# Block sizes 6, 10, 16 in place of 4, 9, 19 in a graph-attention and quantile kernel

## The chip, the cores and the metric

The kernel runs on one core of a Trainium2 chip. A core has a matrix engine (PE, with its weight loads shown as PEld), a vector engine (DVE), a scalar engine (ACT), GpSimd (POOL), and a queue that only issues transfers (SP). The engines run side by side and wait for one another through semaphores. The metric is device time in microseconds, lower is better: the median of three runs of the kernel before is 4632.38 us (4607.63 to 4632.42).

## The reference

There are 4096 nodes of 128 features and a 4096 x 4096 adjacency matrix of which about one entry in 128 is set, some 32 neighbours a row. Two layers are computed.

```python
# layer 0: graph attention with 8 heads, then ELU, a projection, ELU, residual and layer norm
Wh = einsum('nd,hde->hne', nodes, W)
e = leaky_relu(f1[:, :, None] + f2[:, None, :], 0.2)        # f1 = Wh.a1, f2 = Wh.a2
att = softmax(where(adj > 0, e, -9e15), axis=-1)
h = elu(einsum('hnm,hmd->hnd', att, Wh))
x = layernorm(nodes + elu(concat(h) @ W1 + b1))
# layer 1: of each node's neighbours one or two are removed by their rank; for each feature the
# quantiles 0.25, 0.5 and 0.75 over the rest are averaged
agg = 0.5 * mean_of_quantiles + 0.5 * x
out = agg @ W.T + b + x
```

## The kernel before, in words

The rows are worked on in 32 tiles of 128 nodes. The kernel never forms the 4096 x 4096 attention. It finds each node's neighbours as a list of up to 64 indices and gathers the neighbours' rows.

**Search.** `neighbours` (line 568) reads a tile's adjacency rows in two halves by the ACT queue, turns them into signs on ACT, forms sortable keys on PE (lines 625 and 628) and picks the largest ones on DVE, eight at a time: `eights` over chunks of 128 columns (line 592), then eight rounds of `best` (lines 597 and 599). Line 643 is the last step of a tile. `complete_records` (line 649) then finishes the lists of a group of up to four tiles. The function is a generator: it yields `pieces_of(n)` pieces (line 564), which the caller deals out among other work.

**Ranking and blocks.** The nodes of a block of tiles are sorted by their number of neighbours. `rank_by_count` (line 704) works out ranks, and `store_records` (line 391) gives the scatters on the POOL queue that write each node's record (list, count, own index, attention terms, row) to its rank in DRAM. Sorted, the nodes of a tile have nearly equal counts, so a tile needs as many gather slots as its largest count. `CAPS` (line 44) holds that limit for each tile of a block; a count above it raises a flag (line 805), for which a general and much longer path (lines 501 to 503) computes everything again. `BLOCKS` (line 53) holds the blocks' sizes, `TURNS` (line 56) the order in which a block's tiles are taken.

**Attention.** For a sorted tile, `read_lists` (line 796) reads the records back by SP and transposes the lists into index columns. `layers` (line 90) cuts the limit, rounded up to a multiple of four, into layers of 32, 32, 16, 8 or 4 slots. `fetch_rows` (line 847) issues one indirect gather on POOL for every slot (128 rows each) into buffers `G` of 16 slots, six of them. `attend` (line 873) computes scores and Exp (line 894), the denominators (lines 901 and 916), spreads the weights (line 932), multiplies them with `G` on PE (line 944), and does the projections and the norm; `keep_x1` scatters the result.

**Order.** The instruction order of DVE, PE, ACT and POOL is written by hand from line 398 on. The first block is searched before anything else. Then, for each block, `step` (line 357) issues the gathers of one tile, the attention of the tile before it, and between these a quota of pieces of the next block's search. Before a block's last tile the next block's search ends and its ranks are computed; that block's record scatters go among the last tile's gathers. In the last block there is no search: all nodes are ranked together, scatters to `all_d` lie among the gathers of most tiles, and the lists of layer 1 are made in the last four tiles.

**Sort.** The second half gathers the neighbours' layer-0 rows by the lists of all nodes and runs a selection network on DVE (line 1155) for the quantiles; lines 455 to 497. It uses the limits of the entry `32` of `CAPS`, which stay as they are.

Of the kernel before, what the change touches and what calls it, by code (L numbers as in the profile page):

```python
# [41 lines left out]


CAPS = {
    4: [29, 33, 37, 60],
    9: [26, 28, 30, 32, 33, 35, 37, 40, 61],
    19: [24, 26, 27, 28, 29, 30, 30, 31, 32, 33, 33, 34, 35, 36, 37, 38, 40, 42, 62],
    32: [
        23, 24, 25, 26, 27, 27, 28, 29, 29, 30, 30, 30, 31, 31, 32, 32,
        33, 33, 34, 34, 35, 35, 36, 36, 37, 37, 38, 39, 40, 41, 44, 63,  # L50
    ],
}
BLOCKS = [4, 9, 19]


TURNS = {4: range(4), 9: range(9), 19: [0, 1, 2, 3, 18, 4, 5, 6, 7, *range(9, 18), 8]}

CAP = CAPS[NT]
LOW = [
# [142 lines left out]
def scatter(nc, rows, src, idx):  # L202
    return nc.gpsimd.indirect_dma_start(  # L203
        out=rows,
        out_offset=bass.IndirectOffsetOnAxis(ap=idx, axis=0),
        in_=src,
        in_offset=None,
    )
# [9 lines left out]
def kernel(  # L218
# [18 lines left out]
    xt_d = dram.tile([N + P, XW], F32, name="xt_d")  # L237
    recs_d = [dram.tile([n * P, REC], F32, name=f"rec{n}_d") for n in BLOCKS]
    all_d = dram.tile([N, REC1], F32, name="all_d")
# [72 lines left out]
    def search(t0, n):  # L312
        return neighbours(
            tc, adjp, cp, kp, rec, num, adj, t0, n, parts, markb, oneb, bad, jp1, pidx
        )

    for _ in search(0, BLOCKS[0]):
        pass
# [26 lines left out]
    def prepare(b, i, t0):  # L345
        n = BLOCKS[b]
        i = TURNS[n][i]
        return read_lists(tc, attp, recs_d[b], i, CAPS[n][i], t0 + i, bad, narrow)
# [42 lines left out]
    def store_records(b, t0, ranks):  # L391

        return [
            (recs_d[b], rec[:, t0 + i, :], ranks[:, i : i + 1]) for i in range(BLOCKS[b])
        ]

    t0 = 0
    with tc.manual_schedule(engines=ORDERED):
        ranks = rank_by_count(tc, cp, kp, num, jp1, before, oneb, 0, BLOCKS[0])
        for v in store_records(0, 0, ranks):  # L400
            scatter(nc, *v)
        for b, n in enumerate(BLOCKS):
            last = b == len(BLOCKS) - 1
# [1024 lines left out]
```

## Time and profile before

| | |
|---|---|
| Median of three runs | 4632.38 us |
| Profiled execution, its own time | 3702.95 us (span 3701.2 us) |
| DVE busy | 2746.5 us, 74% |
| POOL busy | 2421.0 us, 65% |
| PE busy | 1228.3 us, 33% |
| Gathers of attention (`G`) | 1180, mean 996 ns |
| Gathers of the sort (`vals`) | 1024, mean 1027 ns |

The profiled execution is much shorter than the timed ones. Lines of the profile name an engine, an operation, what it writes and reads, how often, the busy time, the mean time of one, and the engine's idle time before it with what ended most of that. `L944` is line 944 of the kernel. A row of the view by stretches has the stretch, its length, each engine's busy time with its instruction count, the granted clock of PE, the transfer engines' share and their rate. A row of the waits has who waited, for whom, microseconds in all, how often, and the longest.

### The profile page before, as it was taken

What the parts mean: (1) busy time and instruction counts of PE and PEld (TensorE: products, weight loads), DVE (VectorE), ACT (ScalarE), POOL (GpSimd) and SP (SyncE); (2) the same over time, 40 slices, a digit from 0 to 9 for tenths busy, and PEclk for the clock granted to TensorE, in tenths of its full rate; (3) what the DMA queues carried; (4) which work ended last, traced back from release to release, by engine and by line L of the source; (5) the groups of instructions that cost most, each with busy time, mean ns of one, the idle gap of its engine ahead of it and who ended that gap; (6) DMA issues with size and microseconds to landing.
All of it is one profiled execution on the core that took longest, in us unless ns stands there. A gap on an engine that the chain in (4) does not pass through costs nothing. (4 is left out here: it accounts for less than half of the span.)

```text
span 3701.2 us, 23191 instructions
## 1 busy us (share of the span) xinstructions
PE 1228.3 (33%) x5433; PEld 936.3 (25%) x5433; DVE 2746.5 (74%) x7565; ACT 403.4 (11%) x603; POOL 2421.0 (65%) x2388
## 2 busy tenths in 40 slices
PE   6483767773673544454450000000000000000011
PEld 2043544453562443444440000000000000000011
DVE  8774688782541222127637999999999999999998
ACT  3121222220120111111110000000000000000000
POOL 1657674467777777777747777677657565667630
PEclk9975676655575555565555555555555555555555
DMA  6432544322222221222211111111111111111100
GB/s 211 156 99 67 182 137 136 128 72 62 59 54 55 53 55 52 53 66 57 55 33 49 47 47 46 43 46 46 37 38 48 36 42 40 44 44 49 42 19 3
DMA packets 110291, 241.33 MB, mean 65 GB/s; under 512 B 46976, under 2 KB 63360, under 8 KB 101952
## 3 DMA queue, kind: packets, MB, share of 16 engines
q0 software_dynamic: 76160, 160.24, 15.5%
q10 hardware_dynamic: 9360, 67.18, 5.2%
q1 hardware_dynamic: 24624, 12.34, 1.4%
q8 instruction: 45, 0.74, 0.1%
q14 instruction: 102, 0.84, 0.1%
HBM read 228.44 MB, written 11.15 MB: 65 GB/s over the span
## 5 line engine op out<-in xcount | busy, mean ns | idle before, releaser
L194 POOL DMA_INDIRECT G<-xt_d,idx x1180 | 1174.8, 996 | 478.8 <-issue 336.4
L194 POOL DMA_INDIRECT vals<-x_d,idx x1024 | 1052.1, 1027 | 337.6 <-issue 298.5
L1155 DVE TENSOR_TENSOR work<-work 128x512 f32<-128x512 f32 (+6 forms) x1405 | 961.0, 714 | 0.4
L1174 PE MATMUL st_ps<-dg,goal 128*128 128x128 f32 x286 | 71.2, 426 | 1645.3 <-DVE goal L1155 1574.9
L1155 DVE TENSOR_TENSOR work<-work,work 128x512 f32<-128x512 f32 (+5 forms) x958 | 606.4, 658 | 0.7
L1174 PEld LDWEIGHTS st_ps<-dg,goal 128*128 128x128 f32 x286 | 63.2, 322 | 1651.7 <-issue 1650.8
L944 PE MATMUL y<-wide,G 128*128 128x32 f32 (+3 forms) x2360 | 460.3, 371 | 23.9 <-DVE wide L932 23.9
L944 PEld LDWEIGHTS y<-wide,G 128*128 128x128 f32 x2360 | 440.2, 286 | 47.5 <-DVE wide L932 26.3
L887 DVE TENSOR_TENSOR z<-G,f1x 128x128 f32<-128x128 f32 (+2 forms) x92 | 29.9, 335 | 471.5 <-DMA G<-xt_d,idx 467.3
L592 DVE MAX8 first<-key 128x8 f32<-128x128 f32 x1024 | 227.8, 282 | 108.4 <-PE key L628 108.3
L203 POOL DMA_INDIRECT out_dram<-o,own_i x32 | 45.6, 1425 | 297.4 <-ACT o L1200 277.8
L625 PE MATMUL key<-sgn,markb 128*128 128x512 bf16 x256 | 141.6, 554 | 162.3 <-DVE first L592 108.9
L1126 DVE COPY junk<-still 128x1 f32<-128x1 f32 x1295 | 194.7, 150 | 0.0
L901 PE MATMUL small<-z,own 128*4 128x32 f32 (+3 forms) x436 | 50.2, 284 | 380.6 <-ACT z L894 380.6
L1155 DVE TENSOR_TENSOR work<-vals 128x1024 f32<-128x1024 f32 (+8 forms) x140 | 138.8, 1009 | 46.4 <-DMA vals<-x_d,idx 46.1
L586 ACT ACTIVATE sgn<-adj_t 128x2048 bf16<-128x2048 int32 x64 | 122.0, 1907 | 340.7 <-PE key L625 304.5
L1173 ACT ACTIVATE dg<-ident,wt 128x128 f32<-128x128 f32 x143 | 47.5, 394 | 957.2 <-PE st_ps L1174 956.8
L916 PE MATMUL rz<-rden,ownT 4*128 4x32 f32 (+3 forms) x436 | 104.7, 411 | 117.3 <-DVE rden L912 96.0
L628 PE MATMUL key<-parts,oneb 64*128 64x512 bf16 x256 | 140.4, 549 | 6.3 <-POOL parts L212 6.3
L974 PE MATMUL small<-W_sb,late 128*128 128x128 f32 x512 | 118.7, 425 | 33.5 <-DVE late L971 33.5
L901 PEld LDWEIGHTS small<-z,own 128*4 128x4 f32 x436 | 27.1, 102 | 398.1 <-ACT z L894 385.8
L916 PEld LDWEIGHTS rz<-rden,ownT 4*128 4x128 f32 x436 | 91.9, 302 | 133.5 <-DVE rden L912 68.4
(179 smaller groups left out, 1891.7 us busy)
## 6 DMA issues: line engine op xcount, KB each, us to landing
adj_t<-in_adj_dram ACTq DMA_DIRECT2D x64, 1024.0 KB
G<-xt_d,idx POOLq DMA_INDIRECT x1180
vals<-x_d,idx POOLq DMA_INDIRECT x1024
R<-rec_d SPq DMA_DIRECT2D x128, 26.2 KB
xt_d<-rec SPq DMA_DIRECT2D x4, 544.0 KB
rec<-in_x_dram SPq DMA_DIRECT2D x4, 512.0 KB
W_sb<-in_L_gnn_W_dram SPq DMA_DIRECT2D x2, 512.0 KB
a_b<-in_L_gnn_a_dram SPq DMA_DIRECT2D x2, 512.0 KB
```

The lines of the kernel that those rows point to most:

```text
L194: nc.gpsimd.indirect_dma_start(out=dst, out_offset=None, in_=rows, in_offset=bass.IndirectOffsetOnAxis(ap=idx, axis=0),)
L586: nc.scalar.activation(sgn, adj_t, AF.Sign, accum_out=cnt[:, i : i + 1])
L592: nc.vector.max(first[:, ts(c0 // CW + c, 8)], key[:, ts(c, CW)])
L625: nc.tensor.matmul(key, lhsT=markb, rhs=sgn[:, ts(b, 512)], start=True, stop=False)
L628: nc.tensor.matmul(key, lhsT=oneb[0:64, :], rhs=parts[:, ts(r, 512)], start=False, stop=True)
L901: nc.tensor.matmul(den[0:4, :].rearrange("p (g r h) -> p r g h", r=k // 4, h=H)[:, r], lhsT=own[w][:, ts(r, 4)], rhs=z[:, layer[i] : layer ...
L916: nc.tensor.matmul(rz[:, layer[i] * H : (layer[i] + w) * H], lhsT=ownT[w][:, r, :], rhs=rden.rearrange("p (g r h) -> p r g h", r=k // 4, h ...
L944: nc.tensor.matmul(yf[:, ts(g, c)], lhsT=G[:, col + g - g0, 0:D], rhs=pf[:, ts(g, c)], start=(i == 0 and g % (w // 2) == w // 2 - 1), stop ...
L974: nc.tensor.matmul(o, lhsT=hv[:, h, :], rhs=consts["W1_sb"][:, h, :], start=(h == 0), stop=(h == H - 1))
L1126: nc.vector.tensor_copy(junk, late["still"])
L1155: nc.vector.tensor_tensor(slots_of(dst, (j, c, s, m), size), slots_of(a, (i, c, s, m), size), slots_of(b, (i + d, c, s, m), size), op,)
L1174: nc.tensor.matmul(st_ps[:, u, :], lhsT=goal[:, (j * k + u) * D : (j * k + u + 1) * D], rhs=dg, start=(j == 0), stop=False,)
```

## The change

The three blocks of attention tiles get other sizes, still 32 tiles in sum, with limits and an order of tiles to match.

```diff
 CAPS = {
-    4: [29, 33, 37, 60],
-    9: [26, 28, 30, 32, 33, 35, 37, 40, 61],
-    19: [24, 26, 27, 28, 29, 30, 30, 31, 32, 33, 33, 34, 35, 36, 37, 38, 40, 42, 62],
+    6: [28, 30, 33, 35, 39, 61],
+    10: [26, 28, 30, 31, 33, 34, 36, 38, 40, 61],
+    16: [24, 26, 28, 29, 30, 31, 31, 32, 33, 34, 35, 36, 38, 39, 42, 62],
     32: [
         23, 24, 25, 26, 27, 27, 28, 29, 29, 30, 30, 30, 31, 31, 32, 32,
         33, 33, 34, 34, 35, 35, 36, 36, 37, 37, 38, 39, 40, 41, 44, 63,
     ],
 }
-BLOCKS = [4, 9, 19]
+BLOCKS = [6, 10, 16]
 
 
-TURNS = {4: range(4), 9: range(9), 19: [0, 1, 2, 3, 18, 4, 5, 6, 7, *range(9, 18), 8]}
+TURNS = {6: range(6), 10: range(10), 16: [0, 1, 2, 3, 15, 4, 5, 6, *range(8, 15), 7]}
```

Everything else follows from these tables: how many tiles are searched before the first gather, how many pieces of search go into a step, how many slots each tile gathers.

## The prediction

> **What bounds the kernel now.** I read the page's engine shares first (DVE 74%, POOL 65%: shares of stages with different limits), then cut the span where POOL, GpSimd's queue, changes its job: first gather of block 4 (113), of block 9 (362), of block 19 (929), last gather (1884), first gather of the sort (1922). Busy time by engine in each stretch:
>
> ```profile
> core 0: us, PE busy (x) PEld busy (x) DVE busy (x) ACT busy (x) POOL busy (x), PEclk, DMA share, GB/s
> 0.00:113.00 113.00, 59.43 (x168) 25.30 (x168) 81.38 (x315) 32.47 (x86) 19.56 (x28) 1.00 0.57 188
> 113.00:362.00 249.00, 151.46 (x485) 81.32 (x486) 176.18 (x704) 46.95 (x48) 173.31 (x178) 0.77 0.35 108
> 362.00:929.00 567.00, 377.03 (x1572) 251.46 (x1572) 401.90 (x1509) 134.40 (x141) 360.12 (x365) 0.62 0.38 119
> 929.00:1884.00 955.00, 491.02 (x2550) 449.56 (x2549) 350.09 (x1065) 121.97 (x134) 731.98 (x727) 0.58 0.21 56
> 1922.00:3701.00 1779.00, 125.56 (x542) 107.35 (x542) 1723.82 (x3944) 59.18 (x186) 1131.86 (x1088) 0.52 0.14 40
> ```
>
> The sort (last row) is DVE's: 1724 of 1779 us busy. The change doesn't touch it. The first row is the head: a search of four tiles with no gather to run beside it. The middle three are attention. POOL's gathers in block 9's stretch and in block 19's (count, then busy us and mean ns of one, then POOL's idle time before them and what ended it):
>
> ```profile
> L194 POOL DMA_INDIRECT G<-xt_d,idx x337 | 332.1, 985 | 195.0 <-issue 93.2 <-PE y L944 78.0 <-DVE v L1002 14.5
> L194 POOL DMA_INDIRECT G<-xt_d,idx x676 | 680.8, 1007 | 206.0 <-issue 194.7 <-DMA G<-xt_d,idx 5.5 <-DMA all_d<-rec,ranks 3.7
> ```
>
> A gather costs about 1.0 us plus 0.305 us of issue (93.2/306), so 1.29 to 1.31 us. 727 operations at 1.31 fill block 19's 955 us: there POOL alone sets the pace. In the two earlier blocks it also waits. The waits of POOL, by stretch (head; block 4; block 9 twice):
>
> ```profile
> POOL rec_d L203 <- DVE ranks L768: 72.4, 1, 72.4
> ...
> POOL G L194 <- PE y L944: 21.7, 1, 21.7
> ...
> POOL G L194 <- PE y L944: 78.0, 6, 32.5
> POOL G L194 <- DVE v L1002: 14.5, 1, 14.5
> ```
>
> These are waits for a free G buffer (six, of 16 gathered rows): a tile's attention must read G (line 944) before POOL may refill it. They sum to 114 us; with a 2.3 us one of the same kind, 116. That is all a change under the blocks can win. In block 9 the reason is the other stream, DVE and PE in their written order, with an attention step and a share of the search in each. Ends of search tiles in the head (L643), then the Exp that opens an attention step (L894):
>
> ```profile
> 49.52 0.18 DVE L643 TENSOR_SCALAR rec<-rec 128x64 f32<-128x64 f32 x1
> 64.98 0.18 DVE L643 TENSOR_SCALAR rec<-rec 128x64 f32<-128x64 f32 x1
> 80.78 0.18 DVE L643 TENSOR_SCALAR rec<-rec 128x64 f32<-128x64 f32 x1
> ...
> 443.01 0.39 ACT L894 ACTIVATE z<-z 128x224 f32<-128x224 f32 x1
> ...
> 783.97 0.47 ACT L894 ACTIVATE z<-z 128x320 f32<-128x320 f32 x1 [1.55 <-DVE z L893]
> ...
> 1018.18 0.39 ACT L894 ACTIVATE z<-z 128x224 f32<-128x224 f32 x1 [17.19 <-DVE z L893]
> 1047.37 0.39 ACT L894 ACTIVATE z<-z 128x224 f32<-128x224 f32 x1
> ```
>
> A search tile takes 15.6 us in the head. Six steps of block 9, each with 22 search pieces, take 341 us: 56.8 each. A step with no search takes 29.2 (1018 to 1047).
>
> **What the Trainium skill says.** "Perfetto Trace Analysis", section "DMA Instruction — SWDGE (GPSIMD)": the span shown for a GpSimd DMA ends when its descriptors are made, not when data has moved. So 1.3 us is a rate of issue, and the 128 rows land later; the trace agrees (tiles' first DVE reads wait 390 us in all for G's landing). "SBUF — State Buffer", section "SBUF: two separate sides": DVE and GpSimd share a port pair as an exclusive lock, and descriptor writing can be shut out. In this profile I see little of it: gathers of the sort, beside a DVE that is 97% busy, take 1027 ns, those of attention 996. Whether an execution without a profile looks the same, no run here shows, and it matters below.
>
> **The change, part by part.** Slots rounded up to fours sum to 168+336+676 = 1180 before and 236+372+572 = 1180 after. So the gathers are as many as before, and so are the scatters (32 each of records, x1, and all_d). Only where things lie changes.
>
> *Head, added.* Two more tiles searched before the first gather: 2 x 15.6 = 31.2. The records are completed in groups of three and three instead of one of four: one more group; such a group took 6.6 us in block 4 (291.5 to 298.2). Two more record scatters, which stand 2.7 us apart there (98.3, 101.2, 103.8, 106.5): 5.4. Nothing hides any of these: POOL has no index list yet. The ranking's extra doubling step is under 0.5. Sum 43 us; bounds 35 (the second group overlaps the last tile) and 52 (it lengthens the DVE pace too, and the further adjacency loads come late).
>
> *Step lengths, changed.* Pieces of a search of n tiles: 8(n+1) plus 3 for each group: 89, 175 before; 97, 148 after. Block 4 had 30 pieces a step, block 9 22; block 6 will have 20 and block 10 16.4. Between 29.2 at none and 56.8 at 22, a straight line gives 1.255 us a piece, so 54.3 at 20 and 49.8 at 16.4. At 30 it gives 66.9, and block 4 shows 68 (164 to 232), so the line holds past its end.
>
> *Block 9, now block 10.* Test of the method on before: eight steps of 56.8 = 454. POOL's eight tiles before the last one have 272 gathers and 8 x1 scatters: 280 x 1.29 = 361. The difference of 93 is what POOL should wait; the profile shows 94.8 (block 9's waits above plus 2.3). After: the stream is furthest ahead of POOL's need after seven steps, 7 x 49.8 = 349 against 228 gathers and 7 scatters, 235 x 1.29 = 303: 46 us of waits. The last two tiles (41 operations, 53 us each) are again longer than a step. So 95 becomes 46. If the line bends (DVE alone is busy 46.6 of each 56.8), steps are 47 and the waits 26.
>
> *Block 4, now block 6.* Before, three steps (51, 68, 78) ran 61 us over the gathers beside them (40, 46, 50) and POOL waited 21.7; the other 40 the buffers, empty at first, took up. After: about 48, then 54, 54, 53, 53 and a ranking of 9 make 271, less the 9 that lie beside the last tile 262, against 174 x 1.29 = 225: 37 over, about what the buffers take. I put 5 us, bounds 0 and 22.
>
> *Block 19, now block 16.* POOL-bound before (waits 0) and after: four all_d scatters a tile instead of three lie in the same queue and are as many in sum. The lists of layer 1 keep their last four tiles, of 40, 40, 44 and 32 slots both times. Cost zero, hidden under gathers; were that cover gone, they'd be late by one step, 40 us.
>
> *Narrow layers.* 33 instead of 36, four SP loads and about five small DVE operations fewer each (some 1.5 us of DVE, in the shadow of gathers): zero, bounds -5 and 0.
>
> Sum in the profile's own time: +43 - (116 - 46 - 5) = **-22 us**, on 3702.95 (span 3701.2). The median of the timed runs is 4632.38, 929 us longer than the profiled execution, and nothing in the profile says where these lie. I take the difference over unscaled: 4632 - 22 = **4610**.
>
> **The rivals.**
> *B, slower: gathers are the bound already, without a profile.* If the missing 929 us lie partly in GpSimd's descriptors, say 0.3 us more for each gather, POOL no longer waits for buffers: a step of block 9 has 35 operations, so at 56.8/35 = 1.62 us the waits to be won are nil. Then only the head remains: +43, or +54 if DVE and loads there stretch as the whole does (4632/3703 = 1.25): 4675 to 4686. It decides from about 1.45 us an operation, where the waits won (105 - 45 x pace by the sums above) fall to the 43 the head costs. For it: the shared port, and 25% of time unaccounted. Against: 1.3 us in every stage of this profile, whatever DVE does.
> *C, faster: the waits vanish almost wholly.* With fewer pieces DVE and PE wait less for one another, steps of block 10 fall to 44, under most tiles' gathers; 10 us of waits stay: 43 - 106 = -63: 4569. For it: DVE's 82% and PE's 73% in block 9's steps, so part of a step is waiting of one for the other. Against: 29 us of a step is a chain without search.
> *D, a limit is broken.* A tile whose neighbour count is above its limit in the new table sends the kernel into the general path, many times longer. Counts of the reference's adjacency, sorted within each new block, stay at or below every limit (nearest: equal), so I give it nothing.
>
> **How the numbers follow.** Forecast 0.45 (its own range 4590 to 4640), B 0.33, C 0.22. One per cent, 46 us, is about what a measurement can tell from no change (the three runs lie 25 us apart). Faster by over 1% (under 4586): most of C and a corner of the forecast, 0.20. Slower by over 1% (over 4679): the part of B in which the head stretches, with delays that block 6 may add, 0.22. The rest, 0.58. Range: C's 4569 with its bound on narrow layers, to B's 4686: 4564 to 4686.
>
> **What would show it.** In the profile after: first gather at 156 (148 to 165); POOL's waits for y at L944 about 50 us in all instead of 100, none in the last block; steps of block 10 near 50 us; last gather at about 1862 instead of 1884; the sort as long as before, 1779. The forecast is wrong if the waits stay above 75 us, if the head grows by over 52, or if timed runs and profile move in different directions, which would be B.

## The result and the profile after

Over 19 runs each the kernel after takes 4594.25 us (median, 4557.86 to 4624.55) and the kernel before 4613.9 us (4579.41 to 4658.33). The ratio is 0.9952 with a 95% interval of 0.9928 to 0.9976: 20 us, or half a per cent, faster. Wherever an interval is given, here and below, executions of a second, slower state (over 1.5% above the fastest of the same kernel) are left out.

The execution behind the first profile of the kernel before (3703 us) was some 20% shorter than every timed run of that kernel since (4531 to 4662 us); so from here on the kernel before is read from its second profile, the run `b_look`, with a span of 4624.3 us.

The view by stretches of the kernel after, cut at the first gather of blocks 6, 10 and 16 and at the end of attention:

```profile
core 0: us, PE busy (x) PEld busy (x) DVE busy (x) ACT busy (x) POOL busy (x), PEclk, DMA share, GB/s
0.00:149.00 149.00, 77.90 (x200) 28.80 (x200) 108.88 (x453) 41.02 (x94) 21.47 (x30) 1.00 0.54 172
149.00:616.00 467.00, 201.56 (x784) 128.73 (x786) 212.93 (x808) 63.85 (x66) 231.46 (x242) 0.73 0.24 72
616.00:1379.00 763.00, 382.16 (x1600) 263.88 (x1600) 364.15 (x1325) 125.07 (x132) 388.92 (x402) 0.58 0.28 84
1379.00:2503.00 1124.00, 467.88 (x2266) 440.31 (x2267) 326.70 (x1019) 116.84 (x125) 614.57 (x628) 0.55 0.16 41
2503.00:4579.00 2076.00, 127.23 (x542) 108.79 (x542) 1737.13 (x3944) 59.16 (x186) 1159.75 (x1088) 0.51 0.12 35
```

POOL's gathers on the page of the kernel after, its waits for `y` in all, and the same in the stretches of blocks 6, 10 and 16:

```profile
L194 POOL DMA_INDIRECT G<-xt_d,idx x1180 | 1144.2, 970 | 1014.1 <-PE y L944 581.3
```
```profile
POOL G L194 <- PE y L944: 581.3, 25, 46.5
...
POOL G L194 <- PE y L944: 162.0, 6, 46.5
...
POOL G L194 <- PE y L944: 215.7, 9, 29.1
...
POOL G L194 <- PE y L944: 203.6, 10, 26.8
```

Two things are to be seen. The head is 149 us: it grew by 36, inside the forecast's bounds (35 to 52) and below its 43. And POOL waits for `y` in every block, the last one too: 581 us where the forecast expected about 50. A gather still costs what it did (970 ns, and 305 ns of issue before the next). The forecast of 22 us has come out; the waits it was built on are of another size.

### The profile page after: what moved, and what is told of

It is laid out like the page before. It is cut to its first block, busy times and chain, and to the rows that moved or that the text cites. A ratio compares the mean times of both kernels' runs of the same rounds, so it can differ in the third digit from the quotient of the medians.

```text
span 4578.7 us, 23068 instructions
## 1 busy us (share of the span) xinstructions
PE 1256.7 (27%) x5392; PEld 970.5 (21%) x5395; DVE 2749.8 (60%) x7547; ACT 405.9 (9%) x603; POOL 2416.2 (53%) x2388
## 5 line engine op out<-in xcount | busy, mean ns | idle before, releaser
L194 POOL DMA_INDIRECT G<-xt_d,idx x1180 | 1144.2, 970 | 1014.1 <-PE y L944 581.3
L194 POOL DMA_INDIRECT vals<-x_d,idx x1024 | 1075.6, 1050 | 334.5 <-issue 303.8
L944 PE MATMUL y<-wide,G 128*128 128x32 f32 (+3 forms) x2360 | 481.4, 376 | 159.0 <-issue 142.7
L944 PEld LDWEIGHTS y<-wide,G 128*128 128x128 f32 x2360 | 464.4, 294 | 178.7 <-issue 155.0
L911 DVE TENSOR_SCALAR rden<-small 4x256 f32<-4x256 f32 x32 | 13.1, 409 | 583.1 <-remote 289.2
L963 PE MATMUL hT<-late,W_sb 128*128 128x128 f32 x512 | 111.5, 406 | 199.2 <-ACT late L957 153.1
L963 PEld LDWEIGHTS hT<-late,W_sb 128*128 128x128 f32 x512 | 104.3, 310 | 212.1 <-ACT late L957 159.2
L625 PEld LDWEIGHTS <-markb 128*128 128x128 bf16 x256 | 33.3, 130 | 497.5 <-issue 173.8
```

Source lines behind the costliest of these rows:

```text
L194: nc.gpsimd.indirect_dma_start(out=dst, out_offset=None, in_=rows, in_offset=bass.IndirectOffsetOnAxis(ap=idx, axis=0),)
L625: nc.tensor.matmul(key, lhsT=markb, rhs=sgn[:, ts(b, 512)], start=True, stop=False)
L944: nc.tensor.matmul(yf[:, ts(g, c)], lhsT=G[:, col + g - g0, 0:D], rhs=pf[:, ts(g, c)], start=(i == 0 and g % (w // 2) == w // 2 - 1), stop ...
L963: nc.tensor.matmul(hT[:, ts(h, P)], lhsT=consts["W_sb"][:, h, :], rhs=yT[:, h, :], start=True, stop=True)
```

## The experiments

**A second profile of both kernels** (no edit).

> The kernel before once more, for a second profile of it. If the stages of the first profile are typical (head 113, block 4 249, block 9 567, block 19 955, sort 1779 us), this one repeats them within 1%, and the span is near 3700 us. If the timed runs are made as the profile of the kernel after is (span 4579, sort 2076, attention 2354 us), the span is 4580 to 4640 us, with the head still near 113 us, attention near 2400 and the sort near 2076 us.

> The kernel after once more. The same stages as in its first profile are expected within 2%: first gather at 149 us, last gather near 2420 us, sort 2076 us. Forecast's theory: the head is 36 to 43 us longer than in the kernel before, and attention after the head 55 to 70 us shorter.

The kernel before by stretches, in its second profile:

```profile
0.00:115.00 115.00, 59.44 (x168) 25.29 (x168) 81.48 (x315) 32.47 (x86) 19.60 (x29) 1.00 0.58 185
115.00:474.00 359.00, 150.15 (x485) 81.56 (x486) 176.11 (x702) 46.94 (x48) 172.84 (x179) 0.82 0.27 75
474.00:1234.00 760.00, 385.49 (x1555) 249.05 (x1554) 399.15 (x1496) 130.50 (x137) 355.20 (x365) 0.58 0.30 89
1234.00:2416.00 1182.00, 482.06 (x2418) 447.17 (x2418) 324.20 (x997) 120.72 (x129) 714.26 (x725) 0.55 0.20 45
2416.00:2499.00 83.00, 55.13 (x266) 49.99 (x265) 37.74 (x112) 15.51 (x18) 4.86 (x5) 0.58 0.02 5
2499.00:4624.00 2125.00, 124.00 (x542) 106.31 (x542) 1739.82 (x3944) 59.16 (x186) 1156.37 (x1088) 0.51 0.13 34
```

Busy times are those of the first profile; the lengths are not. Block 4 takes 359 us instead of 249, block 9 760 instead of 567, block 19 1182 instead of 955, the sort 2125 instead of 1779. What fills the difference is idle time. Of the two outcomes expected of this run the second came, a span like that of the timed runs. In the first profile PE's next key follows at once on the DVE instructions it waits for (start, duration, instruction):

```profile
121.94 0.89 DVE L592 MAX8 first<-key 128x8 f32<-128x128 f32 x4 [0.45 <-PE key L628]
...
122.91 0.10 PEld L625 LDWEIGHTS <-markb 128*128 128x128 bf16 x1 [0.44 <-DVE first L592]
```

In the second profile of the same kernel, while POOL gathers:

```profile
191.26 0.88 DVE L592 MAX8 first<-key 128x8 f32<-128x128 f32 x4
...
198.62 0.10 PEld L625 LDWEIGHTS <-markb 128*128 128x128 bf16 x1 [8.46 <-remote]
```

DVE ends at 122.83 and PE starts at 122.91: 0.08 us. Here DVE ends at 192.14 and PE starts at 198.62: 6.5 us. ("remote" is a wait whose end the profile can put down to no instruction, because none ended just before.)

The last block, where no search lies, shows longer ones. Below are the first matmuls of an attention step (the denominators) and the DVE instruction that waits for them; then what DVE waited for from the start of that block to the end of attention, two lines of the first profile and three of the second:

```profile
1498.26 2.22 PE L901 MATMUL small<-z,own 128*4 128x128 f32 x28
...
1529.38 0.41 DVE L911 TENSOR_SCALAR rden<-small 4x256 f32<-4x256 f32 x1 [36.93 <-remote]
```
```profile
DVE z L887 <- DMA G<-xt_d,idx: 467.1, 40, 25.9
...
DVE rden L911 <- PE small L901: 17.1, 10, 7.1
...
DVE rden L911 <- remote: 353.1, 9, 55.2
DVE rden L911 <- PE small L901: 158.2, 5, 60.6
...
DVE z L887 <- DMA G<-xt_d,idx: 26.6, 3, 23.6
```

PE ends at 1500.48, DVE starts 28.9 us later, and in between no instruction of PE, DVE or ACT runs while POOL issues 20 gathers and three scatters. In the first profile DVE waits here for gathered rows, as in a block that POOL bounds; in the second it waits at L911, and POOL then waits for `y`.

The trace also has the times at which each engine's semaphore counts up. DVE's wait at L911 is for PE's alone, and that one counts at 1529.36; PE starts at 198.62 when DVE's has counted at 198.57. So it is the count that is late, not a transfer that is waited for. Up to the sort, the second profile has 2414 counts of these two semaphores, of which 193 stand over 1 us behind the last instruction that raises them, the longest 72 us; in the first profile none of 2982 does. Both profiles hold 23191 instructions, so no lost instruction explains it. Late counts aren't all of the loss: PE also stands still 142 us between matmuls at L944 with no wait that the profile names, where the first profile has none.

The two kernels' second profiles end attention at 2496 and 2493 us, the sorts take 2125 and 2048: a sort that no edit touches varies by more than the effect. So later runs leave it out. After the head, attention is 39 us shorter in this pair (2381 and 2342), not the 55 to 70 of the forecast's theory.

**Attention without its gathers** (left out: the gathered rows; the values are zeros).

```diff
-                G, col = ap.tile([P, 16, XW], F32, name="G", bufs=6), 0
+                G, col = still_G, 0
...
-            gather(nc, G[:, col, :], xt_d, idx[:, g : g + 1])
```

> The kernel before without the gathers of attention: the buffers G are one constant tile of zeros, so lists, search, weights and products are all done, on other values, and POOL only scatters. If POOL's pace and its waits for buffers set attention, head and attention fall from 1884 us (first profile) to the stream's own sum: 113 + 3 steps (197) + 9 of 57 + 19 of 29, about 1380 us, or 500 us less. If the 929 us by which the timed runs exceed the first profile come from what gathers do to the other engines, most of the attention's part of them goes too: a time near 3500 us. If the stream is slow by itself, the time stays above 4200 us.

> The kernel after without the gathers of attention, as in the kernel before without them. Forecast's theory: no wait for buffers is left to be won, so only the head (+43) and the fewer pieces beside attention (264 to 245, at 1.255 us: -24) remain: 19 us SLOWER than the kernel before without gathers. Rival (the gain does not come from POOL's waits but from work saved in the stream): it stays faster by about 20 us.

Measured: 3627.8 us against 4577 for the whole kernel before on that chip, a ratio of 0.7923 (0.7854 to 0.7992): 950 us for 1180 gathers. The sort's first gather stands at 1579 us, where attention of the kernel before ended at 2496. That is near the second expectation (3500 us); the first, the sort's start at 1380 us, is missed by 199. Late counts, waits for buffers and POOL's own pace are all in the 950 us. Up to the sort, neither kernel without gathers has a count of PE's or DVE's semaphore over 1 us late; in the sort, which keeps its gathers, waits for "remote" are still there. So the lateness goes with the gathers. The run takes out their issue, their transfers and the waits for them together, and does not part these. Of the 923 us by which the second profile is longer than the first, 577 lie before the sort (2499 instead of 1922) and 346 in it.

With blocks 6, 10, 16 it is 3583.97 us, 44 less by medians (47 with an interval of 40 either way by means), not 19 more. In the profiles the sort starts at 1513 instead of 1579: 66 us earlier. (The kernel after was profiled in the longest of its four executions, but what is longer there is the sort, 2109 against 2048 us.) Exp by Exp (line 895 here is line 894 of the kernel before), first in block 9 of the kernel before, then in block 10 of the kernel after:

```profile
425.56 0.39 ACT L895 ACTIVATE z<-z 128x224 f32<-128x224 f32 x1
482.13 0.39 ACT L895 ACTIVATE z<-z 128x224 f32<-128x224 f32 x1
542.10 0.42 ACT L895 ACTIVATE z<-z 128x256 f32<-128x256 f32 x1 [1.53 <-DVE z L894]
...
651.60 0.44 ACT L895 ACTIVATE z<-z 128x288 f32<-128x288 f32 x1
```
```profile
498.34 0.39 ACT L895 ACTIVATE z<-z 128x224 f32<-128x224 f32 x1
546.79 0.39 ACT L895 ACTIVATE z<-z 128x224 f32<-128x224 f32 x1
597.48 0.42 ACT L895 ACTIVATE z<-z 128x256 f32<-128x256 f32 x1 [2.67 <-DVE z L894]
...
731.26 0.44 ACT L895 ACTIVATE z<-z 128x288 f32<-128x288 f32 x1
```

Four steps of 56.5 us against five of 46.6. The stream of DVE and PE is itself shorter with thin search; POOL's waits for buffers are not needed for it, since here there are none.

**Attention alone, the sort left out** (zeros are written for the output). The runs after this one are compared with `b_ns`, and all use this edit.

```diff
-        fetched = fetch_unit(order[0])
...
-        write_out(*done)
+        zero = sp.tile([P, D], F32, name="zero", bufs=1)
+        nc.vector.memset(zero, 0.0)
+        for t in range(NT):
+            nc.sync.dma_start(out[ts(t, P), :], zero)
```

> The kernel before without the sort (it writes zeros instead), so that head and attention are timed alone, without the scatter of a 2000 us sort over them. By the second profile of the kernel before, attention ends at 2496 us: a time near 2500 us. It is the base of the three that follow.

> The kernel after without the sort. Forecast's theory (43 us of head against waits that thinner search takes away): 22 us less than the kernel before without the sort. If what was measured of the whole kernels comes from the sort or by chance: the same within 5 us. By the second profiles (attention ends at 2496 and at 2493): 3 us less.

Measured: 2552.67 us (2545.85 to 2569.93) and 2527.04 us (2510.56 to 2538.05): 26 us less by medians, 32 with an interval of 14 either way by means. The gain is attention's, and of the size forecast. Where, by stretches, before and after:

```profile
0.00:115.00 115.00, 59.43 (x168) 25.29 (x168) 81.75 (x315) 32.41 (x86) 19.91 (x29) 1.00 0.58 185
115.00:475.00 360.00, 153.53 (x485) 83.64 (x486) 175.75 (x702) 43.79 (x46) 171.06 (x179) 0.82 0.26 75
475.00:1239.00 764.00, 391.35 (x1553) 254.10 (x1552) 400.56 (x1501) 133.49 (x139) 355.25 (x364) 0.57 0.30 88
1239.00:2441.00 1202.00, 489.73 (x2419) 455.26 (x2420) 322.69 (x993) 121.00 (x130) 710.69 (x725) 0.56 0.20 44
```
```profile
0.00:151.00 151.00, 77.88 (x200) 28.80 (x200) 109.06 (x454) 41.03 (x94) 21.48 (x30) 1.00 0.54 170
151.00:628.00 477.00, 200.22 (x785) 127.16 (x786) 214.53 (x816) 63.87 (x66) 238.11 (x250) 0.71 0.26 72
628.00:1401.00 773.00, 391.68 (x1617) 271.92 (x1616) 363.54 (x1323) 128.35 (x134) 382.58 (x398) 0.58 0.29 82
1401.00:2405.00 1004.00, 391.61 (x1987) 364.35 (x1987) 286.84 (x900) 98.15 (x107) 608.93 (x618) 0.56 0.20 45
```

POOL's waits in a stretch are its length less POOL's busy time less 0.305 us of issue for each operation. That gives 134, 298 and 270 us before (702 in all), and 163, 269 and 207 after (638): 64 less, against 36 more of head. (The part that the profile puts down to `y` at L944, the sign that the prediction named, does not fall: 574 and 579 us here, 551 and 553 in the second profiles. What falls has other names.) For each tile they fall from 33 us to 27 in the blocks that carry search, and stay at 14 and 13 in the last one.

**Other blocks** (the tables alone).

```diff
-BLOCKS = [4, 9, 19]
+BLOCKS = [4, 10, 18]
...
+BLOCKS = [8, 11, 13]
```

> Blocks of 4, 10 and 18 tiles, without the sort: the head stays at four tiles, the middle block alone is thinned (18 tiles of search over ten tiles of attention instead of 19 over nine); 1180 slots as before. Forecast's sums: block 10 has 18.4 pieces a step, its waits fall from 95 to 63, block 4 loses 12 more: 20 us less than 4, 9, 19, as good as 6, 10, 16. If a longer head is what is needed for the gain (block 4 too dense with ten tiles of search on 168 slots): between 6 us less and 15 us more.

> Blocks of 8, 11 and 13 tiles, without the sort: the head grows by four tiles instead of two, and search beside attention is thinnest; 1180 slots as before. Forecast's sums: head +80, waits 116 down to 15: 21 us less than 4, 9, 19, and no better than 6, 10, 16. If a search tile costs 18 us in the head and not under 7 us beside gathers, as the stage lengths of the second profiles give: 5 to 10 us more than 4, 9, 19. If POOL's waits were nothing to win: 80 us more.

Measured: 2522.04 us for 4, 10, 18 (it has 1176 slots, not 1180 as the expectation says: 5 us of POOL) and 2507.99 us for 8, 11, 13. By means that is 34 us (interval 12 either way) and 46 us (14) under the kernel before. So thinning the middle block alone is worth what 6, 10, 16 is, though the head stays as it was. The rival for 4, 10, 18 (between 6 us less and 15 more) falls; so does the reading by stage lengths for 8, 11, 13 (5 to 10 us more), and the forecast's sum of 21 us less was too small there. In 8, 11, 13 the stretches are as follows; the last line is block 10 of 4, 10, 18:

```profile
0.00:185.00 185.00, 96.28 (x232) 32.10 (x232) 134.00 (x564) 48.93 (x102) 23.39 (x32) 1.00 0.50 163
185.00:776.00 591.00, 255.84 (x1033) 176.41 (x1034) 251.72 (x928) 80.85 (x84) 309.69 (x324) 0.65 0.26 71
776.00:1540.00 764.00, 391.51 (x1669) 288.44 (x1668) 334.28 (x1180) 123.28 (x129) 416.15 (x428) 0.58 0.28 78
1540.00:2401.00 861.00, 321.27 (x1655) 298.30 (x1655) 253.45 (x822) 79.68 (x87) 499.60 (x510) 0.56 0.19 43
...
484.00:1278.00 794.00, 423.14 (x1635) 285.30 (x1634) 395.82 (x1467) 133.14 (x140) 386.64 (x401) 0.56 0.30 86
```

The head is 70 us longer than in 4, 9, 19, and the waits 182, 217 and 206: 605 in all, 97 less. Each tile waits 23 and 20 us in the blocks with search.

**The head alone.**

```diff
     for _ in search(0, BLOCKS[0]):
         pass
+    for _ in search(BLOCKS[0], EARLY):    # EARLY = 2; block 4 then searches the other seven
+        pass
```

> The head alone: blocks 4, 9, 19 as before, but two of block 9's tiles are searched in the head too, so that block 4 carries seven tiles of search instead of nine; without the sort. Forecast's theory: head +36 to +39 (two search tiles and one more group of records, no more scatters), block 4's wait for buffers less by 22: 15 us more than the kernel before without the sort. If a search tile costs as much beside gathers as in the head: no change. If thinning block 4 is worth what blocks 6, 10, 16 gained: 25 us less.

Measured: 2559.08 us (2549.03 to 2571.72), 3 us more than `b_ns` by means with an interval of 15 either way. But this run and the next were timed on another chip than `b_ns`. As a ratio to the whole kernel before, timed beside each, it is 0.5533 (0.5506 to 0.5560) against 0.5565 (0.5533 to 0.5597), which would be some 15 us less. So the times don't decide among the three expectations; the stretches say more.

```profile
0.00:145.00 145.00, 77.97 (x200) 28.81 (x200) 107.73 (x451) 41.10 (x94) 19.58 (x28) 1.00 0.55 175
145.00:469.00 324.00, 125.29 (x452) 73.23 (x454) 146.13 (x566) 38.90 (x40) 170.88 (x178) 0.84 0.26 70
```

The head grew by 30 us for two tiles and one more group of records (the forecast had 37.8 for these), and block 4 shrank by 36. So, in one profile of each, the eighth and ninth search tile of block 4 cost at least as much beside gathers as they do in the head.

**All search in the head.**

```diff
-    for _ in search(0, BLOCKS[0]):
-        pass
+    for t0, n in ((0, 4), (4, 9), (13, 19)):
+        for _ in search(t0, n):
+            pass
...
-                pieces, left = search(t0 + n, BLOCKS[b + 1]), pieces_of(BLOCKS[b + 1])
+                pieces, left = iter(()), 0
```

> All 32 tiles are searched in the head and none beside attention; blocks 4, 9, 19 as before, without the sort. Then every attention stage shows its waits with no search in it. Stage lengths so far put a search tile at 18 us in the head and at 7 to 9 us beside gathers (237 us for 28 tiles in the kernel before): first gather near 620 us, attention after it 2210 us, 2810 to 2840 us in all against 2553. POOL's waits per tile then near 14 us in all blocks, as in block 19. Forecast's theory, which has no waits where no search lies: waits zero, 1660 us after the first gather, 2300 us in all.

Measured: 2676.06 us (2664.04 to 2681.99). Both expected times miss: the head is cheaper than 18 us a tile, and the waits don't vanish. That POOL waits about as long for each tile in all blocks came nearly as expected: 11, 16 and 14 us.

```profile
0.00:480.00 480.00, 312.54 (x612) 71.03 (x612) 441.89 (x2074) 141.30 (x194) 19.56 (x28) 1.00 0.48 156
480.00:751.00 271.00, 75.58 (x360) 70.84 (x361) 44.61 (x128) 15.14 (x16) 171.32 (x178) 0.81 0.21 49
751.00:1365.00 614.00, 244.76 (x1251) 227.19 (x1253) 132.36 (x323) 59.31 (x65) 360.00 (x365) 0.57 0.20 45
1365.00:2558.00 1193.00, 466.59 (x2395) 434.82 (x2397) 322.72 (x986) 117.25 (x127) 711.01 (x724) 0.56 0.20 45
```

28 more tiles cost the head 365 us, 13 each. With no search beside it block 4 takes 271 instead of 360, block 9 614 instead of 764: search cost 89 and 150 us there, 10 and 8 a tile on average, while the last two of block 4 had cost 18 each. So the cost of a search tile beside attention rises with how many share an attention tile. The middle blocks of all runs agree. An estimate: with 614/9 = 68 us for a tile of attention without search, what is left of block 9's 764 us is 8 us for each of its 19 search tiles; of block 10's 794 us in 4, 10, 18, 6 us for each of 18; of block 10's 773 us in 6, 10, 16, 6 us for each of 16; of block 11's 764 us in 8, 11, 13, 1 us for each of 13. And POOL still waits 45, 143 and 261 us, 449 of 702, with no search at all.

**8, 11, 13 in the whole kernel** (its tables, with the sort).

> Blocks of 8, 11 and 13 tiles in the whole kernel, with the sort. Without the sort it took 45 us less than 4, 9, 19 and 19 less than 6, 10, 16. If that carries over: 4555 to 4575 us against 4600, a ratio of 0.990. If the sort's beginning depends on how attention ends, the gain may be lost: 4600 us.

Measured: 4582.24 us against 4625.54 beside it, ratio 0.9912 (0.9868 to 0.9957). It beats the kernel before. Its interval overlaps that of 6, 10, 16; without the sort it is 14 us ahead of it by means, with an interval of 13 either way.

## Why the prediction was right, and where its steps were not

The forecast was 22 us less, by 43 of head against 65 of waits. Measured: 20 us less in the whole kernels; 36 of head against 64 of waits in the sort-less ones. The time and the balance held. The place and the origin of the waits did not. By the prediction's own signs its account of the waits is wrong: they were to stay under 75 us, with none in the last block, and POOL waited 581 us for `y`, 204 of them there; the last gather was to come at 1862 us and came at 2419.

- **Head, added.** +36 instead of +43: 113 or 115 to 149 or 151. Two tiles with one more group took 30 us, not 37.8, and 28 more took 13 us each; the 15.6 read between the first three is too much.
- **Step lengths.** The line gave 56.8 and 49.8 us. Without gathers they are 56.5 and 46.6: the line bends, as the lower bound allowed. With gathers, and late counts, block 9 takes 764/9 = 85 us a tile.
- **Block 9, now block 10.** 95 to 46 was forecast, 298 to 269 measured. The test of the method on the first profile (93 against 94.8) belongs to that one execution, in which no count came late.
- **Block 4, now block 6.** 22 to 5 was forecast, 134 to 163 measured: 27 us a tile instead of 33, with two tiles more.
- **Block 19, now block 16.** This is the step that failed: "POOL-bound before (waits 0) and after". Measured 270 to 207, and since the other two blocks' changes cancel (+29, -29), the whole difference of 64 us stands here. In place of waiting for gathered rows, DVE waits there at L911, in the second profile of the kernel before 353 us of it for late counts of PE, and POOL waits for both in turn. A tile of the last block waits about 14 us with no search in sight, and three tiles have left it for blocks where a tile waits 27. That the total came out at the forecast's 65 is luck: the forecast had all of it in blocks 9 and 4, where -29 and +29 were measured.
- **What thinning does.** The forecast held POOL's buffers to be the place where thin search pays. The pair without gathers speaks against that: the forecast's theory has 19 us more there, and 44 to 47 less was measured (66 in the profiles). What pays is that search beside attention costs more a tile where it is dense. 4, 10, 18 and 8, 11, 13 agree with that, the second over the forecast's sum.
- **Rival B** said that unprofiled gathers are slow and POOL the bound. Gathers keep their 1.28 us; it is the other engines that lose time while POOL gathers, and so POOL waits more, not less. (A sum of it is off: by 105 - 45 x pace the waits won fall to 43 at 1.38 us an operation, not at 1.45. Nothing rests on it.) **Rival C** (waits nearly gone) is refuted. **D** did not happen.

Open is why a count comes late while POOL gathers, and why one execution was free of it. The runs show that it goes with the gathers; whether their issue or their transfers do it was not tried.

## What to carry to other kernels

Where background work is dealt out among the steps of a pipeline, its cost per piece rises with its density, so give it more steps to lie beside, as long as the serial head that this lengthens costs less: 8, 11, 13 still gained, all search in the head lost over 100 us. Where between them the best lies was not tried. Check a profile's own time against the timed runs before reading waits from it: a profile 20% shorter than the timed runs gave the right busy times, but put the waits in the wrong stage. When a long stage that is not touched varies by more than the effect, leave it out and time the rest.

## What was not expected of the hardware

While GpSimd issues gathers, the semaphore by which one engine tells another that it is done can count late: 6.4 us after DVE's end and 28.9 us after PE's in the lines shown from the second profile, up to 72 us; in the first profile and in the runs without gathers, nowhere over 1 us before the sort. So two streams side by side can take far longer than either needs. Without gathers the other engines reach the sort after 1579 us. POOL's own work, with the head before it but without any wait, is 115 + 1237 + 387 = 1739 us in `b_ns` (head, busy, issue); together they take 2441. The section "SBUF: two separate sides" of the Trainium skill's "SBUF — State Buffer" tells of DVE shutting GpSimd out of a shared port, so that descriptors can't be written. That is not what these runs show: gathers keep 0.95 to 1.05 us beside a busy DVE (1050 ns in the sort after), and DVE's busy time is the same in both profiles of the kernel before (2746.5 and 2758.5 us). What grows is the time between the instructions of the other engines.
